# The norm's sums by way of DRAM, two transfers a chunk, and the roots one part of a turn later

## The chip, the cores and the metric

The kernel runs on one core of one Trainium2 chip. The metric is the device time of a whole execution in microseconds (us).

## The reference

Four images of 96 channels and 128 x 128 pixels go through two layers. The first layer is a state-space block: a projection to 192 channels, a depthwise convolution, SiLU, four scans along the pixels, and then a norm over the 192 channels of each pixel, a projection back to 96 channels and the residual. The second layer is a block of convolutions with an attention among channels. The change lies in the norm that ends the first layer. Cut to that, the reference is:

```python
yn = jnp.moveaxis(ym, 1, -1)                 # ym: the sum of four scans, [image, 192, 128, 128]
mu = yn.mean(-1, keepdims=True)
var = yn.var(-1, keepdims=True)
yn = (yn - mu) * jax.lax.rsqrt(var + 1e-05) * ln_w + ln_b
yn = jnp.moveaxis(yn, -1, 1)
return jnp.einsum('bdhw,cd->bchw', yn, out_w) + out_b[None, :, None, None]
...
x = x + _L0_conv_ref(_gn(x), ...)
```

## The kernel before

**The norm.** `ssm_output` makes one image's norm in 16 chunks of 1024 pixels (`SN`), each of two halves of 512 (`CH`). The mean over the channels is folded into the output weights `outws`, so that only the factor 1/sqrt(var + eps) of each pixel is needed beside the projection. A chunk goes these ways:

- `load_y` (L951, L953): SP loads the chunk's 192 channels from `yms` as `y` (128 channels) and `yr` (64 channels, the two halves one below the other).
- `squares` (L959): ACT makes the squares of `y` (part 0) and of `yr` (part 1).
- `sums` (L970): PE sums the values and the squares over the channels, with a matrix of 1/192 of 32 columns. The four results, mean and mean square of each half, stand in one PSUM bank at partitions 0, 32, 64 and 96.
- `rows` (L982, L984, L989): ACT copies the bank to `st` (L984 in image 0, L982 in the others, where the pixels are put into another order on the way), and then four DMAs from ACT's queue bring the four rows of 512 to the tile `mq`, 32 partitions x 2 x 32, where the arithmetic on them is short.
- `inverse` (L996 to L998): three short operations of DVE make the variance. `roots` (L1002): ACT takes the root. `back` (L1006, L1008, L1010): DVE takes the reciprocal, POOL's queue stores it to the DRAM tile `rd`, and SP loads the residual `xr`. `spread_out` (L1016): POOL's queue loads it as `r`, 96 partitions all alike.
- `projected` (L1023, L1028): PE multiplies the chunk by the output weights, into two banks. `scaled` (L1037, L1039): DVE multiplies a bank by `r`, which frees it. `added` (L1045, L1047): POOL adds `xr`, to which ACT had added the bias (L1092). `counted` (L1051): DVE's statistics for the next layer. L1098: SP stores the chunk to `xnew`.

**A turn.** The loop at the end of `ssm_output` has 18 turns. Turn c works on three chunks: the new one c (squares, sums, rows), the middle one c - 1 (from the inverse to `r`) and the old one c - 2 (projection to store). A turn has six parts, each ended by a `yield` with a cost.

**The order.** `ssm_output` is a generator. `co_run` runs two generators by turns, by their costs: `left`, and beside it `light` or `last`. The norm of image 0 runs as `left` beside the last part of the scan (`ssm_scan`: softplus L676, exponentials L809, DVE's scan L837, L854, L858, POOL's products L833 and L866). The norms of images 1, 2 and 3 run as `light` beside the convolutions of the image before (L2169, L1477 and others). `in_order(first)` ties every engine's instructions from the first projection on, image 0's norm included, to the order in which the program emits them. What is emitted after it, the norms of images 1 to 3 with it, is arranged by the framework, which takes the order of emission as a priority and puts an instruction where it takes it to be ready. Each engine then runs its own queue in order, and an instruction that waits holds up all behind it.

**Buffers.** `mq`, `r` and `xr` have two buffers each, `st` one, `y` and `yr` three. The PSUM pool of the norm has three banks in image 0 and two in images 1 to 3; `projected` takes two and `sums` one.

Of the kernel before, what the change touches and what calls it, by code (L numbers as in the profile page):

```python
# [9 lines left out]
F32 = mybir.dt.float32  # L10
# [10 lines left out]
CH = 512  # L21
# [11 lines left out]
TN = W // TW  # L33
# [38 lines left out]
def kernel(  # L72
# [26 lines left out]
    nc = tc.nc  # L99
# [4 lines left out]
    dram = ctx.enter_context(tc.tile_pool(name="dram", bufs=2, space=DRAM))  # L104
# [45 lines left out]
    for q in range(2):  # L150
        at = 32 * q + 16
# [137 lines left out]
    def bank(ps):  # L289

        return ps.tile([128, CH], F32, name="bank", tag="bank")

    def part(ps, *shape):
        n = 1
        for d in shape[1:]:
            n *= d
        t = bank(ps)[: shape[0], :n]
        return t if len(shape) == 2 else t.rearrange("p (a b) -> p a b", b=shape[2])
# [636 lines left out]
    def ssm_output(b, yms, xnew, stats, ps, side, turned):  # L935

        with tc.tile_pool(name="c2", bufs=2, side=side) as p2:
            xb = x[b].rearrange("c h w -> c (h w)")
            rd = dram.tile([L], F32, name="rd")
            ys, sums_of, near, made = {}, {}, {}, {}

            def load_y(c):
                if c < NS:
                    y, rest = ys[c] = [
                        p2.tile([128, n], F32, name=m, bufs=3) for m, n in (("y", SN), ("yr", CH))
                    ]  # L950
                    nc.sync.dma_start(y, yms[0:128, bass.ts(c, SN)])  # L951
                    for h in range(2):
                        nc.sync.dma_start(  # L953
                            rest[64 * h : 64 * h + 64], yms[128:192, bass.ts(2 * c + h, CH)]
                        )

            def squares(c, j):
                sq = p2.tile([128, CH if j else SN], F32, name=f"sq{j}")
                nc.scalar.activation(sq, ys[c][j], AF.Square)  # L959
                sums_of[c, j] = sq  # L960

            def sums(c, j):
                sq = sums_of.pop((c, j))
                if j == 0:
                    sums_of[c] = bank(ps)
                pm = sums_of[c]
                for g in range(4):
                    rhs = sq if g % 2 else ys[c][j]
                    p = slice(64 * (g // 2), 64 * (g // 2) + 64) if j else slice(0, 128)
                    nc.tensor.matmul(  # L970
                        pm[32 * g : 32 * g + 32],
                        lhsT=mean192[p],
                        rhs=rhs[p, :] if j else rhs[:, bass.ts(g // 2, CH)],
                        start=(j == 0),
                        stop=(j == 1),
                    )
            def rows(c):
                st = p2.tile([128, CH], F32, name="st", bufs=1)
                pm = sums_of.pop(c)
                if turned:  # L980
                    to = st.rearrange("p (h j t) -> p h j t", j=TW, t=TN)
                    nc.scalar.copy(to, turned_view(pm))  # L982
                else:
                    nc.scalar.copy(st, pm)  # L984
                mq = made[c] = p2.tile([SN // TN, 2, TN], F32, name="mq")
                for i in range(2):
                    for h in range(2):
                        at = 32 * i + 64 * h
                        nc.scalar.dma_start(  # L989
                            mq[16 * h : 16 * h + 16, i],  # L990
                            st[at : at + 1].rearrange("p (a f) -> p a f", f=TN),
                        )

            def inverse(c):
                m, q = made[c][:, 0], made[c][:, 1]
                nc.vector.tensor_mul(m, m, m)  # L996
                nc.vector.tensor_sub(q, q, m)
                nc.vector.tensor_scalar(q, q, 0.0, None, ALU.max)  # L998

            def roots(c):  # L1000
                q = made[c][:, 1]
                nc.scalar.activation(q, q, AF.Sqrt, bias=eps[0 : SN // TN])  # L1002

            def back(c):
                q = made.pop(c)[:, 1]
                nc.vector.reciprocal(q, q)  # L1006
                to = rd[bass.ts(c, SN)]
                nc.gpsimd.dma_start(to.rearrange("(p f) -> p f", f=TN), q)  # L1008
                xr = p2.tile([C, SN], F32, name="xr")
                nc.sync.dma_start(xr, xb[:, bass.ts(c, SN)])  # L1010
                near[c] = xr, to

            def spread_out(c):
                xr, to = near[c]
                r = p2.tile([C, SN], F32, name="r")
                nc.gpsimd.dma_start(r, to.partition_broadcast(C))  # L1016
                near[c] = xr, r

            def projected(c):
                po = [part(ps, C, CH) for _ in range(2)]  # L1020
                y, rest = ys.pop(c)
                for h in range(2):
                    nc.tensor.matmul(  # L1023
                        po[h], lhsT=outws[:, 0], rhs=y[:, bass.ts(h, CH)], start=True, stop=False
                    )
                for h in range(2):
                    p = slice(64 * h, 64 * h + 64)
                    nc.tensor.matmul(  # L1028
                        po[h], lhsT=outws[p, 1], rhs=rest[p], start=False, stop=True
                    )  # L1030
                return po

            def scaled(c, h, po):
                r = near[c][1][:, bass.ts(h, CH)]
                if turned:
                    v = r.rearrange("p (h j t) -> p h j t", t=TN, j=TW)
                    nc.vector.tensor_mul(v, turned_view(po), v)  # L1037
                else:
                    nc.vector.tensor_mul(r, po, r)  # L1039

            def added(c, h):
                xr, r = (t[:, bass.ts(h, CH)] for t in near[c])
                if turned:
                    v = r.rearrange("p (h j t) -> p h j t", t=TN, j=TW)
                    nc.gpsimd.tensor_add(v, v, turned_view(xr))  # L1045
                else:
                    nc.gpsimd.tensor_add(xr, r, xr)  # L1047

            def counted(c, h):
                t = near[c][turned]  # L1050
                nc.vector.bn_stats(stats[:, 2 * c + h], t[:, bass.ts(h, CH)])  # L1051

            for c in range(3):
                load_y(c)
            yield 2.0
            for c in range(NS + 2):
                new, old = c < NS, c - 2 if c >= 2 else None
                mid = c - 1 if 1 <= c <= NS else None
                if old is not None:
                    po = projected(old)  # L1060
                if mid is not None:
                    inverse(mid)
                if new:
                    squares(c, 0)
                yield 1.2
                if mid is not None:
                    roots(mid)
                if old is not None:
                    scaled(old, 0, po[0])
                if new:  # L1070
                    squares(c, 1)
                yield 1.4
                if mid is not None:
                    back(mid)
                if old is not None:
                    added(old, 0)
                    scaled(old, 1, po[1])
                if new:
                    sums(c, 0)
                yield 1.4  # L1080
                if new:
                    sums(c, 1)
                if old is not None:
                    added(old, 1)
                    counted(old, 0)
                    load_y(c + 1)
                yield 1.4
                if new:
                    rows(c)
                if mid is not None:  # L1090
                    xr = near[mid][0]
                    nc.scalar.activation(xr, xr, AF.Identity, bias=outbs)  # L1092
                    spread_out(mid)
                if old is not None:
                    counted(old, 1)
                yield 1.4
                if old is not None:
                    nc.sync.dma_start(xnew[:, bass.ts(old, SN)], near.pop(old)[turned])  # L1098
                yield 1.4
# [176 lines left out]
    def turned_view(v):  # L1276

        return v.rearrange("p (h t j) -> p h j t", t=TN, j=TW)
# [1310 lines left out]
    at = Attention(psl, d1, d2, pm)  # L2589
# [108 lines left out]
```

## Time and profile before

| what | value |
|---|---|
| median of three runs | 6406.59 us (6383.12 to 6412.63) |
| the profiled execution | 6409.68 us, its span 6407.8 us |
| PE, DVE, ACT, POOL busy | 82%, 73%, 59%, 51% of the span |
| norm of image 0, first to last copy `st` | 2105.6 to 2329.2 us |
| norms of images 1, 2, 3, first to last copy `st` | 3248.3 to 3496.4, 3964.1 to 4182.4, 4789.6 to 5005.4 us |
| DMAs `mq<-st` on ACT's queue | 256, 2.0 KB each |

PE is the matmul engine (TensorE), PEld its weight load, DVE the VectorE, ACT the ScalarE, POOL the GpSimd, SP the SyncE, which here only issues DMAs. A "q" behind an engine means its instruction queue. In a table by stretches each engine has its busy us and, in brackets, its number of instructions; then come the granted share of PE's clock, the share of the DMA engines in use and GB/s. A row of waits names who waited for whom, the us in total, how many times, and the longest. A row of a timeline has start, duration, engine, line, operation, output<-inputs, shapes, and in square brackets the idle time of the engine before it and what ended it. A row with three numbers between slashes gives the least, median and greatest duration in ns; then the first and last start in us.

### The profile page before, as it was taken

The page shows a single profiled execution, that of the slowest core. Times are in us where ns is not written, and L with a number is a line of the kernel's source. Part 1 is how long each engine was busy: PE and PEld are TensorE (multiplying, and loading weights), DVE is VectorE, ACT ScalarE, POOL GpSimd, SP SyncE. Part 2 cuts the span into 40 slices and gives each one's busy share as a digit, 9 for nine tenths or more (in the row PEclk, how much of TensorE's full clock was granted, in tenths as well). Part 3 has the DMA queues.
Part 4 walks back from the last instruction along what each step waited for, and adds up shares of the span by engine and source line. Part 5 has one row for each costly group of instructions (what it writes and reads, how often), then busy time and mean ns, then how long its engine had stood idle before and what let it go on. Part 6 is the DMA issues. An engine that isn't in the chain of part 4 may idle for free. (4 is left out here: it accounts for less than half of the span.)

```text
span 6407.8 us, 76468 instructions
## 1 busy us (share of the span) xinstructions
PE 5253.4 (82%) x23264; PEld 2254.8 (35%) x23264; DVE 4699.9 (73%) x7132; ACT 3759.4 (59%) x4770; POOL 3238.6 (51%) x2476
## 2 busy tenths in 40 slices
PE   6889988987888643989988588977888877889888
PEld 2333322322222111444433234345333444345553
DVE  4247878988989768989844686468774687988767
ACT  1247767787787666777622465466644665545642
POOL 1326757978879554979822234436304365022310
PEclk9899989998999765999999799989989888999989
DMA  6766777775675766676667686665776656967668
GB/s 155 175 160 189 198 199 199 214 221 163 198 202 171 202 183 207 196 213 179 182 185 195 166 228 163 195 169 156 214 199 184 175 149 165 245 167 180 191 168 221
DMA packets 897706, 1205.30 MB, mean 188 GB/s; under 512 B 230644, under 2 KB 745642, under 8 KB 884816
## 3 DMA queue, kind: packets, MB, share of 16 engines
q1 hardware_dynamic: 866640, 1145.36, 65.5%
q0 software_dynamic: 16336, 38.51, 2.3%
q10 hardware_dynamic: 14320, 16.54, 0.9%
q8 instruction: 187, 3.06, 0.2%
q14 instruction: 223, 1.83, 0.1%
HBM read 777.82 MB, written 345.62 MB: 175 GB/s over the span
## 5 line engine op out<-in xcount | busy, mean ns | idle before, releaser
L633 PE MATMUL bank<-y,wp 128*128 128x512 f32 (+3 forms) x3584 | 1310.9, 622 | 83.8 <-DMA y<-y 41.0
L866 POOL TENSOR_TENSOR y<-y,dl 128x1024 f32<-128x1024 f32 x384 | 1058.5, 2757 | 263.0 <-DVE dl L858 240.3
L833 POOL TENSOR_TENSOR dl<-dl,u 128x1024 f32<-128x1024 f32 x384 | 1008.8, 2627 | 253.1 <-ACT dA L809 121.1
L854 DVE TENSOR_TENSOR_SCAN dA<-dA,pBC 128x512 f32<-128x512 f32 x768 | 981.6, 1278 | 30.7
L2169 PE MATMUL bank<-y,wn 128*64 128x384 f32 (+5 forms) x2408 | 680.1, 507 | 58.3 <-DMA y<-x1d 34.1
L1477 PE MATMUL two<-ya,wd 128*64 128x192 f32 (+3 forms) x2376 | 582.2, 414 | 174.0 <-ACT odd L1550 65.1
L633 PEld LDWEIGHTS bank<-y,wp 128*128 128x128 f32 (+3 forms) x3584 | 456.2, 168 | 749.3 <-issue 651.1
L858 DVE TENSOR_TENSOR dl<-dA,pBC 128x512 f32<-128x512 f32 x768 | 528.5, 688 | 255.8 <-PE pBC L747 183.8
L747 PE MATMUL pBC<-xr,wbc 60*128 60x512 bf16 (+1 forms) x1536 | 457.8, 404 | 311.5 <-DVE dA L854 239.1
L1938 ACT COPY yb<-ya 64x768 f32<-64x768 f32 (+1 forms) x660 | 537.7, 815 | 195.5 <-PE two L1477 113.8
L676 ACT ACTIVATE dl<-pd,dtb 128x512 f32<-128x512 f32 x768 | 485.5, 684 | 187.9 <-PE pd L747 171.5
L1477 PE MATMUL two<-yb,wd 128*64 128x192 f32 (+3 forms) x2376 | 559.0, 400 | 4.0 <-ACT yb L1938 4.0
L837 DVE TENSOR_TENSOR pBC<-dl,pBC 128x512 f32<-128x512 f32 x768 | 527.5, 687 | 8.8 <-POOL dl L833 7.8
L2169 PEld LDWEIGHTS bank<-y,wn 128*64 128x64 f32 (+3 forms) x2408 | 310.3, 169 | 357.2 <-issue 186.2
L809 ACT ACTIVATE dA<-dl,negA 128x1024 f32<-128x1024 f32 x384 | 420.3, 1141 | 2.3
L1477 PEld LDWEIGHTS two<-ya,wd 128*64 128x64 f32 (+1 forms) x2376 | 262.2, 165 | 370.9 <-ACT odd L1550 75.0
L676 ACT ACT_TABLE_LOAD x248 | 318.2, 1283 | 91.9 <-PE pd L747 79.7
L747 PEld LDWEIGHTS <-wbc 60*128 60x128 bf16 (+1 forms) x1536 | 103.1, 96 | 752.1 <-issue 739.3
L1477 PEld LDWEIGHTS two<-yb,wd 128*64 128x64 f32 (+1 forms) x2376 | 289.7, 167 | 150.5 <-issue 42.1
L1477 PE MATMUL two<-ya,wa 128*96 128x384 f32 (+1 forms) x528 | 231.2, 521 | 72.9 <-DMA ya<-vp 27.0
L1550 ACT COPY odd<-two 128x384 f32<-128x384 f32 (+5 forms) x176 | 115.8, 658 | 291.3 <-PE two L1492 179.1
L1406 POOL TENSOR_TENSOR pl<-x 96x256 f32<-96x256 f32 (+3 forms) x396 | 275.2, 710 | 0.0
(322 smaller groups left out, 9105.4 us busy)
## 6 DMA issues: line engine op xcount, KB each, us to landing
u<-zb SPq DMA_DIRECT2D x192, 1024.0 KB
yms<-y SPq DMA_DIRECT2D x96, 512.0 KB
xn<-xnew SPq DMA_DIRECT2D x128, 384.0 KB
ya<-vp SPq DMA_DIRECT2D x120, 336.0 KB
y<-y SPq DMA_DIRECT2D x128, 258.2 KB
zb<-z SPq DMA_DIRECT2D x64, 512.0 KB
y<-yms SPq DMA_DIRECT2D x64, 512.0 KB
ya<-x1p SPq DMA_DIRECT2D x90, 336.0 KB
```

What stands on the lines that cost most here:

```text
L633: nc.tensor.matmul(blocks(pz[p:e]), lhsT=ws[k][:, d, c : c + e - p], rhs=window(ys[k], at, d, n), start=(i == 0), stop=(i == len(terms) - 1),)
L676: nc.scalar.activation(dst, src, AF.Softplus, bias=bias)
L747: nc.tensor.matmul(p, lhsT=w[rows], rhs=xr[rows, at : at + CH], start=True, stop=True)
L809: nc.scalar.activation(live[m]["dA"], live[m]["dl"], AF.Exp, scale=negA[:, g % 3, k : k + 1])
L833: nc.gpsimd.tensor_mul(t, t, u_view(n))
L837: nc.vector.tensor_mul(p, live[n]["dl"][:, bass.ts(half, CH)], p)
L854: nc.vector.tensor_tensor_scan(h, h, p, init, ALU.mult, ALU.add)
L858: nc.vector.tensor_mul(live[n]["dl"][:, sl], live[n]["dA"][:, sl], live[n]["C", half])
L866: nc.gpsimd.tensor_add(v, v, t.rearrange("p (a b) -> p a b", b=W))
L1477: nc.tensor.matmul(of(to[p:e], r), lhsT=w[:, i, c : c + e - p], rhs=tiles(t[k][PAIR[i]][:, SLOT[i]], o, r), start=(k == 0), stop=False,)
L1938: nc.scalar.copy(yb[k][64 * h - 64 : 64 * h, :, :n], ya[k][0:64, :, h * TN : h * TN + n])
L2169: nc.tensor.matmul(pc[p:e, :n].rearrange("p (h w) -> p h w", w=W), lhsT=w[:, c : c + e - p], rhs=v[:, :, 0:W], start=(i == 0), stop=(i == ...
```

## The change

The sums of a chunk go from `st` to a DRAM tile of 4 x 512 in one DMA, and from there to `mq` in a second one, both on ACT's queue. For that the rows of the bank are put into another order: first the two means, then the two mean squares. There are two such DRAM tiles, taken by turns. In a turn `inverse` moves from part 1 to part 2, `roots` from part 2 to part 3, and `back`, with its reciprocal, its store to `rd` and its load of `xr`, from part 3 to part 4. `spread_out` stays in part 5.

```diff
@@ ssm_output
             rd = dram.tile([L], F32, name="rd")
+            sums_to = [dram.tile([4, CH], F32, name=f"sums{i}") for i in range(2)]
...
                 for g in range(4):
-                    rhs = sq if g % 2 else ys[c][j]
-                    p = slice(64 * (g // 2), 64 * (g // 2) + 64) if j else slice(0, 128)
+                    rhs = sq if g // 2 else ys[c][j]
+                    h = g % 2
+                    p = slice(64 * h, 64 * h + 64) if j else slice(0, 128)
                     nc.tensor.matmul(
                         pm[32 * g : 32 * g + 32],
                         lhsT=mean192[p],
-                        rhs=rhs[p, :] if j else rhs[:, bass.ts(g // 2, CH)],
+                        rhs=rhs[p, :] if j else rhs[:, bass.ts(h, CH)],
...
                 mq = made[c] = p2.tile([SN // TN, 2, TN], F32, name="mq")
-                for i in range(2):
-                    for h in range(2):
-                        at = 32 * i + 64 * h
-                        nc.scalar.dma_start(
-                            mq[16 * h : 16 * h + 16, i],
-                            st[at : at + 1].rearrange("p (a f) -> p a f", f=TN),
-                        )
+                nc.scalar.dma_start(sums_to[c % 2], st[0:128:32])
+                nc.scalar.dma_start(
+                    mq, sums_to[c % 2].rearrange("(i h) (a f) -> (h a) i f", i=2, f=TN)
+                )
...
                 if old is not None:
                     po = projected(old)
-                if mid is not None:
-                    inverse(mid)
                 if new:
                     squares(c, 0)
                 yield 1.2
                 if mid is not None:
-                    roots(mid)
+                    inverse(mid)
                 if old is not None:
                     scaled(old, 0, po[0])
                 if new:
                     squares(c, 1)
                 yield 1.4
                 if mid is not None:
-                    back(mid)
+                    roots(mid)
                 if old is not None:
                     added(old, 0)
                     scaled(old, 1, po[1])
                 if new:
                     sums(c, 0)
                 yield 1.4
+                if mid is not None:
+                    back(mid)
                 if new:
                     sums(c, 1)
```

## The prediction

> **What bounds the kernel now.** I first took the stretches table over the four times in which the norm (`ssm_output`) runs, one for each image: from its first to its last copy of sums (row L984, then L982).
>
> ```profile
> core 0: us, PE busy (x) PEld busy (x) DVE busy (x) ACT busy (x) POOL busy (x), PEclk, DMA share, GB/s
> 2105.00:2340.00 235.00, 153.86 (x464) 31.39 (x461) 155.91 (x217) 146.76 (x169) 121.12 (x89) 0.77 0.71 211
> 3245.00:3505.00 260.00, 220.10 (x832) 80.06 (x832) 101.34 (x225) 75.36 (x120) 58.60 (x58) 0.93 0.69 187
> 3960.00:4190.00 230.00, 209.25 (x1179) 86.28 (x1176) 108.70 (x240) 109.21 (x153) 81.90 (x106) 0.99 0.66 183
> 4785.00:5015.00 230.00, 206.71 (x1113) 83.45 (x1112) 103.51 (x234) 105.99 (x150) 90.90 (x119) 0.96 0.68 192
> ```
>
> Only 955 of 6407.8 us hold any work of this change, so 0.5% (32 us) is 3.4% of the place where it can act, or 0.5 us in each of 64 turns. In images 1 to 3 PE is busy 85 to 91%: PE sets the time there, and a wait on another engine counts only where PE then waits. In image 0 no engine stands out: the waits decide.
>
> ```profile
> PE bank L970 <- ACT sq L959: 54.2, 15, 7.5
> ACT xr L1092 <- DMA mq<-st: 32.2, 10, 5.8
> ACT st L984 <- PE bank L970: 25.4, 12, 3.6
> ```
>
> This is the table of waits from 2105 to 2340. PE waits mainly for the squares that ACT makes. ACT's 146.8 us leave out its DMA issues; 64 of them at 0.602 us (the row below) are 38.5 us more, 185 of 235. So **ACT's queue sets image 0's turn**, 14.9 us (2105.6 to 2329.2 in 15 turns). ACT's timeline shows one turn:
>
> ```profile
> 2206.35 0.58 ACT L984 COPY st<-bank 128x512 f32<-128x512 f32 x1 [2.04 <-PE bank L970]
> 2206.97 2.43 ACTq L989 DMA_DIRECT2D mq<-st  x4
> 2209.50 1.15 ACT L1092 ACTIVATE xr<-xr,outbs 96x1024 f32<-96x1024 f32 x1 [2.56 <-DMA mq<-st]
> 2210.56 1.04 ACT L959 ACTIVATE sq<-y 128x1024 f32<-128x1024 f32 x1
> 2211.62 1.28 ACT L676 ACT_TABLE_LOAD   x1
> 2212.91 1.27 ACT L676 ACTIVATE dl<-pd,dtb 128x512 f32<-128x512 f32 x2
> 2214.20 1.28 ACT L1002 ACT_TABLE_LOAD   x1
> 2215.49 0.32 ACT L1002 ACTIVATE mq<-mq,eps 32x32 f32<-32x32 f32 x1
> 2215.72 0.61 ACT L959 ACTIVATE sq<-yr 128x512 f32<-128x512 f32 x1
> 2218.37 0.59 ACT L984 COPY st<-bank 128x512 f32<-128x512 f32 x1 [2.04 <-PE bank L970]
> ```
>
> ACT is never idle except 2.04 us before the copy `st`, where PE sums the squares it has just made. Before L1092 stand the 2.43 us of four issues. The root stands ahead of the second squares, so its 1.60 us (table load and 0.32) delay them and the sums. Next, the waits table of image 1 (3245 to 3505):
>
> ```profile
> DVE mq L996 <- DMA mq<-st: 65.1, 14, 8.6
> PE bank L970 <- DVE r L1037: 20.7, 6, 7.9
> DVE r L1037 <- DMA r<-rd: 11.2, 4, 3.8
> ```
>
> DVE waits long for the sums, but what reaches PE is only its wait for `scaled` (r L1037), which frees the PSUM bank. The same PE row is 9.8 and 9.0 us in images 2 and 3: 39.5 us together. Read back from those waits on the timeline, DVE had stood at L996 before some of them and at the landing of `r<-rd` before about as many.
>
> **What the Trainium skill says.** "DMA: Bandwidth & Descriptors", section "Two DMAs through the same engine are not ordered": a DMA that reads what another wrote must have its issuing engine wait for the first one's semaphore. The trace agrees: POOL's issue of `r<-rd` waits for `rd<-mq`, 21.4 us in nine times in image 0. So ACT will stand between its two issues. The same page, "Issuing engines are not separate DMA queues": all issuers share the 16 DMA engines, so a small transfer can stand behind SP's. The trace agrees: in its packet records, the last packet of a turn's four `mq<-st` ended 0.80 us at the least after the last issue, 2.10 in image 0's mean, 4.31 at most, 1.50 in the mean of images 1 to 3.
>
> **The change part by part, image 0.** There the issue order is that of the program.
>
> ```profile
> L989 ACTq DMA_DIRECT2D mq<-st x256: 508/602/1947, 2106.2 to 5008.3; - x128
> ```
>
> - Two issues in place of four: 2 x 0.602 = 1.2 us in place of 2.4, so 1.2 less a turn.
> - The wait between them, W, isn't in the trace. From below: the quickest write of like size to DRAM is `rd<-mq`,
>
> ```profile
> L1008 POOL DMA_DIRECT2D rd<-mq x64: 496/518/544, 2114.3 to 5013.6; - x64
> DMA to landing us min/median/max: 1.6/4.2/8.3
> ```
>
> 1.6 us with its 0.5 us of issue, so 1.1. From above: its median less the issue, 3.7. The queue of ACT is hardware and its packets in image 0 ended 2.1 us after the issue; a DRAM landing adds 0.3 (1.1 against 0.8, the two minima), but four rows go in place of 64 pieces. I take W = 2.3. Behind it on ACT wait L1092, both squares, softplus and the exponentials, and PE waits for those.
> - Net on ACT: 2.3 - 1.2 = +1.1 a turn, 16 turns, **+18 us**; bounds -2 and +40.
> - L1092 waits in any case: its rows in the waits table (32.2, 6.5, 3.7, 2.6 and 2.5 us in 15 waits) hold 15 x 2.43 of issue, and the rest, 11 us, is mostly the load of `xr`. W runs beside that: **-8 us** (0 to -11). The load's issue on SP moves one part later with `back`, past SP's rows and stores of the scan; it stood there for its buffer anyway (in the timeline SP issued the store that frees it at 2195.69 and this load at 2201.49, 8 us ahead of L1092), so I count that at nothing; if the cover of 8 us is gone, L1092 waits for it, by at most a part, 2.5 us.
> - The root moves behind the second squares into the 2.04 us hole. Twelve turns have such a hole (25.4 us); 1.5 us each, **-18 us**. From the other side, 0, if a softplus of the scan fills the hole or DVE's inverse is late.
> - The sums' new order lets two matmuls in place of one go before the squares are there. PE's hole of 2 us gets shorter by part of a matmul; the root covers it: nothing.
> - DVE and POOL: the inverse one part later takes away DVE's stand at L996 (15.5 us of waits, and inside the instruction: 2.57 us at 2210.25 where the median is 0.18). DVE is busy 66% and ACT hardly waits for it (4.1 us): nothing. POOL gets `rd<-mq` one part later, so `r<-rd` waits longer for its landing, by about the 2.5 us of a part; POOL is busy 52% and now idles as long at L1008. The scan's POOL products behind it cover with their lead; if that is gone, DVE waits for `dl`.
>
> Image 0: 18 - 8 - 18 = **-8 us**, from -31 to +40.
>
> **Images 1 to 3, 48 turns.** Here the order in the trace is not the program's: r L1037 stands between L996 and L997, which the program emits in a row. So "one part later" may move little. The sums reach SBUF after 0.6 + 1.8 (1.50 + 0.3) + 0.6 + 1.8 = 4.8 us, before 2.4 + 1.5 = 3.9: 0.9 later, against a part of 14.9/6 = 2.5. DVE's waits for them are 65.1 + 8.9, 45.2 + 7.9 and 51.5 + 5.1 = 184 us, 3.8 a turn; 1.6 a turn goes, 77 us, of which PE feels 39.5/184: -16. The factor `r` lands 1 to 2 us later; DVE's waits for it were 11.2 + 9.7 + 11.8 us in twelve turns, eight turns more at 1.5 us, half of it reaching PE: +6. ACT stands some 1.1 us longer, but it idles over half of these stretches, and PE waits for ACT's squares, `odd` and `kt` 19 us in all: +6 at a guess of a tenth of the 53 us. Sum **-4 us**; bounds -40 (all of PE's wait for `scaled`) and +40 (three quarters of ACT's 53 us).
>
> **Sum.** -8 - 4 = -12 us. The profiled execution took 6409.7 us, its span 6407.8, and 2 us lie around it; it is 3 us above the median shown, 6406.6. I subtract from the median: **6395 us**.
>
> **Rivals.**
> 1. *Landing under load becomes ACT's wait* (slower). Place: ACT between its two issues. For it: the landing of 4.2 us at the median, a DMA share of 0.71, a first packet that began up to 3.8 us after the issue. Image 0 +40; in images 1 to 3 PE waits for ACT and for a late `r`, +10: 6457. It decides from W = 2.8 us on, where 1.2 saved and (18 + 8)/16 = 1.6 are used up. Against it: the quickest landings of 1.1.
> 2. *DVE's stand at the sums was on PE's path* (faster). Then nearly all of the 39.5 us goes, and image 0 comes near its -8 with W small: 39.5 + 8 = 47 less: 6359. For it: DVE's 184 us. Against it: `r<-rd` stood before half of those waits.
> 3. *The change doesn't do what it says*: the order of images 1 to 3 puts the inverse right after the sums again, the parts move nothing and the extra trip through DRAM makes `r` late. +10 there and -8 in image 0: 6409.
>
> **How the numbers follow.** 0.5% is about what a measurement of this kernel can tell from no change (the three runs lie 29 us apart). Forecast 0.37, rival 3 0.06, rival 2 0.31, rival 1 0.26. A tenth of the forecast's own range goes over on the faster side and rival 1 may stop short: faster 0.34, same 0.41, slower 0.25. The range goes from a little beyond rival 2, 6347, to rival 1, 6457; forecast's own 6374 to 6438.
>
> **What the profile after would show.** Right: two rows of ACT issues of 64, and ACT idle about 2 us between them; L1002's table load between the second squares and `st`, and the wait `st` <- PE near 5 us; DVE's mq waits down from 184 to about 110 us; image 0's turn at 14.4 us. Wrong: a stand of over 3 us on ACT between the issues, PE waiting for squares for over 54 us, or DVE r <- `r<-rd` doubled to over 65 us.

## The result, and the profile after

The changed kernel takes 6431.69 us in the median of nine runs, the kernel before, on the same chip, 6405.73 us: the ratio is 1.0052, with a 95% interval of 1.0038 to 1.0066. A second measurement of the same kernel (`e9_change_again`) gave 1.0058 (1.0037 to 1.0078). So the change makes the kernel slower by half a per cent, 26 to 37 us, where the forecast had it 12 us faster. The profiled execution took 6430.42 us, its span 6428.6, 20.8 more than before.

In the changed kernel the lines stand elsewhere: squares L960, sums L972, the copy `st` L986 (L984 in images 1 to 3), the two transfers L988 and L989, inverse L995 to L997, root L1001, reciprocal L1005, `rd` L1007, `scaled` L1036 and L1038, bias L1091.

First the table of stretches, over the same four times as before.

```profile
core 0: us, PE busy (x) PEld busy (x) DVE busy (x) ACT busy (x) POOL busy (x), PEclk, DMA share, GB/s
2105.00:2340.00 235.00, 147.60 (x471) 30.18 (x469) 142.52 (x211) 143.94 (x168) 121.30 (x89) 0.77 0.72 208
3245.00:3505.00 260.00, 225.34 (x834) 80.53 (x834) 99.37 (x214) 71.68 (x114) 58.99 (x56) 0.93 0.67 186
3960.00:4190.00 230.00, 200.00 (x1096) 81.63 (x1094) 101.55 (x227) 98.70 (x139) 77.99 (x102) 0.96 0.64 175
4785.00:5015.00 230.00, 205.82 (x1029) 82.59 (x1028) 114.68 (x236) 99.61 (x139) 74.36 (x99) 0.93 0.67 186
```

The reader should look at the number of matmuls. In image 2, 1096 of them fall into 230 us in place of 1179, in image 3 1029 in place of 1113: the same work runs later. In image 0 DVE gets through 211 instructions in place of 217.

The waits of image 0 (2108 to 2347: who waited for whom, us in total, times, the longest):

```profile
PE bank L972 <- ACT sq L960: 50.8, 14, 9.0
ACT xr L1091 <- DMA sums<-st: 47.5, 11, 7.9
ACT st L986 <- PE bank L972: 15.3, 8, 3.3
```

ACT's wait for PE's sums at `st` went from 25.4 to 15.3, as intended, but the row ahead of L1091 went from 32.2 (four issues) to 47.5 (one issue and a stand), with its rows of other causes from 51.0 to 71.5. One turn on ACT's timeline shows the stand:

```profile
2206.90 0.61 ACT L960 ACTIVATE sq<-yr 128x512 f32<-128x512 f32 x1
2207.53 1.28 ACT L1001 ACT_TABLE_LOAD   x1
2208.83 0.32 ACT L1001 ACTIVATE mq<-mq,eps 32x32 f32<-32x32 f32 x1
2209.14 0.59 ACT L986 COPY st<-bank 128x512 f32<-128x512 f32 x1
2209.75 0.50 ACTq L988 DMA_DIRECT2D sums<-st  x1
2215.02 0.31 ACTq L989 DMA_DIRECT2D mq<-sums  x1
2215.43 1.15 ACT L1091 ACTIVATE xr<-xr,outbs 96x1024 f32<-96x1024 f32 x1 [5.71 <-DMA sums<-st]
```

The root stands behind the second squares and in this turn the hole ahead of `st` is gone (no idle time in brackets). Then ACT ends the first issue at 2210.25 and begins the second at 2215.02: a stand of 4.77 us. Over the 16 turns of image 0 this stand is 3.66 us in the mean (1.24 to 6.88). In images 1 to 3 2.4 to 2.6 us lie between the two issues, but in 25 of 48 chunks the framework put other work between them; ACT is idle 1.3 to 2.0 us in the mean just ahead of the second. The issues themselves are shorter than the 0.602 us of before (least, median, greatest in ns):

```profile
L988 ACTq DMA_DIRECT2D sums<-st x64: 501/502/1061, 2109.3 to 5032.5; - x64
L989 ACTq DMA_DIRECT2D mq<-sums x64: 309/322/376, 2111.8 to 5037.2; - x64
```

In image 1 (waits from 3245 to 3515):

```profile
DVE mq L995 <- DMA mq<-sums: 46.1, 12, 8.9
DVE r L1036 <- DMA r<-rd: 24.9, 5, 7.4
PE bank L972 <- DVE r L1036: 14.4, 6, 5.6
```

Over images 1 to 3, in the same three windows of both profiles (3245 to 3515, 3960 to 4215, 4780 to 5060), DVE's waits for the sums fell from 186 to 123 us (46.1, 40.4, 36.5), and its waits for the factor `r` rose from 41 to 85 (24.9, 31.7, 28.2). PE's wait for `scaled` did not move: 38.7 us (14.4, 17.5, 6.8), before 39.5. These are single executions: the seven profiles whose order in these images is that of before (`before`, `e1`, `e6`, `e7`, `e8`, `e15`, `e18`) have 143 to 186 us of waits for the sums, and `before` has the most.

### The profile page after: what moved, and what is told of

The parts are those of the page before. It is cut to its first block, busy times and chain, and to the rows that moved or that the text cites. A ratio compares the mean times of both kernels' runs of the same rounds, so it can differ in the third digit from the quotient of the medians.

```text
span 6428.6 us, 76281 instructions
## 1 busy us (share of the span) xinstructions
PE 5252.6 (82%) x23264; PEld 2253.8 (35%) x23264; DVE 4692.6 (73%) x7132; ACT 3758.9 (58%) x4770; POOL 3241.7 (50%) x2476
## 5 line engine op out<-in xcount | busy, mean ns | idle before, releaser
L2168 PE MATMUL bank<-y,wn 128*128 128x384 f32 (+5 forms) x2408 | 676.0, 506 | 62.9 <-DMA y<-x1d 30.1
L2168 PEld LDWEIGHTS bank<-y,wn 128*128 128x128 f32 (+3 forms) x2408 | 308.3, 168 | 357.2 <-issue 180.3
## 6 DMA issues: line engine op xcount, KB each, us to landing
ya<-vp SPq DMA_DIRECT2D x120, 336.0 KB
ya<-x1p SPq DMA_DIRECT2D x90, 336.0 KB
```

The costliest lines, as they stand in the source:

```text
L2168: nc.tensor.matmul(pc[p:e, :n].rearrange("p (h w) -> p h w", w=W), lhsT=w[:, c : c + e - p], rhs=v[:, :, 0:W], start=(i == 0), stop=(i == ...
```

## The experiments

The theories that the expectations name are these. STAND: ACT's stand between the two transfers costs the time. LATE: the numbers come later (`mq`, then `r` and the load of `xr`). RING: an old chunk's buffers come free too late. ORDER: the framework arranges the instructions of images 1 to 3 anew, and the arrangement it made for the kernel before was a good one. Each run is told by its ratio to the kernel before. Beside it I use the length of a stretch of PE's work between the same two matmuls in every profile, which shows where time was lost; it is worked out from the traces and comes from one execution each.

**Where, and which half.** The whole change in image 0 alone, and in images 1 to 3 alone (`turned` is true there; the diff is that of `e1` against the changed kernel, `e2` has the opposite condition):

```diff
-                nc.scalar.dma_start(sums_to[c % 2], st[0:128:32])
...
+                if not turned:
+                    nc.scalar.dma_start(sums_to[c % 2], st[0:128:32])
...
+                else:
+                    for i in range(2):
+                        for h in range(2):
...
-                    inverse(mid)
+                    (roots if turned else inverse)(mid)
...
-                    roots(mid)
+                    (back if turned else roots)(mid)
```

> The whole change (two transfers by way of DRAM, the sums' order, the parts) in image 0 alone, where the order of issue is that of the program; images 1 to 3 go the way of the kernel before. In the profile after, ACT stood 3.7 us in the mean between its two issues in image 0, and the place had lost 5 us. Theory STAND (ACT's wait between the issues delays what is behind it): +5 us or more, up to +17 if the profile's 5 us were lucky; PE's wait for the squares in image 0 over 54 us. Theory LATE (the loss is that r comes late and holds the PSUM banks in images 1 to 3): within 4 us of the kernel before. Theory ORDER (the framework arranges images 1 to 3 otherwise, by luck): anything within 15 us, by what it rearranges behind image 0.

> The whole change in images 1 to 3 alone; image 0 goes the way of the kernel before. The profile after put about 20 of its 26 us here, 14 of them in image 2. STAND: with the framework's filling between the two issues, +5. LATE: +15 to +25, with DVE's wait for r<-rd at 65 us or more in place of 33. ORDER: a number that doesn't go together with image 0's to make 26.

Measured: 1.0012 (1.0004 to 1.0021) in image 0 alone, 1.0024 (1.0015 to 1.0033) in images 1 to 3 alone. Both places lose; a third of the two lies in image 0. Together they make 0.36%, less than the 0.52 and 0.58% of the whole.

Then the two halves of the change over all images. `e3` has the transfers by DRAM and the order of the sums as in the change, and the parts of before; `e4` has the four transfers and the sums of before, and the moved parts, its whole diff against before:

```diff
-                    inverse(mid)
...
-                    roots(mid)
+                    inverse(mid)
...
-                    back(mid)
+                    roots(mid)
...
+                    back(mid)
```

> The two transfers by way of DRAM with the sums' order that goes with them, and inverse, roots and reciprocal in the parts of the kernel before. STAND: as slow as the whole change or slower, +26 to +45, since the root is ahead of the second squares again and ACT still stands. LATE: less than the whole change, about +10, since a part's delay of r is taken back: DVE's wait for r<-rd falls towards 45 us. ORDER: between 0 and +40.

> Four transfers on chip as before, and inverse, roots and reciprocal one part later. STAND: a gain, 10 to 18 us, from the root in the hole before the copy of the sums in image 0, and DVE no longer standing at the sums. LATE: a loss of about 10, since r comes a part later without the trip. ORDER: between -15 and +15.

Measured: 1.0031 (1.0019 to 1.0042) and 1.0019 (1.0010 to 1.0027). Neither half is free, and 0.31 + 0.19 = 0.50% is about the whole. But each of them also makes the framework arrange images 1 to 3 anew. I counted in the traces the instructions that stand at another place in their engine's order than before (DMA issues left out; an expectation below counts in another way): there `e3` has 359 of DVE and 196 of ACT, `e4` 218 and 148, the change 431 and 238. So these four runs can't tell a step from what the framework makes of it.

**Steps alone, in which images 1 to 3 stay put.** In the kernel before, `e6` issues `spread_out` one part later (the first diff), `e7` has the root behind the second squares (the second), and `e8` the new order of the sums (the third):

```diff
-                    spread_out(mid)
...
+                if mid is not None:
+                    spread_out(mid)
```

```diff
-                if mid is not None:
-                    roots(mid)
...
                 if new:
                     squares(c, 1)
+                if mid is not None:
+                    roots(mid)
```

```diff
-                    rhs = sq if g % 2 else ys[c][j]
+                    rhs = sq if g // 2 else ys[c][j]
```

> The kernel before, with spread_out (POOL's load r<-rd) in part 6 in place of 5; it moves eight rows of POOL in image 0 and nothing else. LATE: DVE's wait for r<-rd in image 0 rises from 5 us towards 25, and the kernel loses 3 to 10 us (1.0005 to 1.0015). STAND: no change.

> The kernel before, with the root behind the second squares within part 2; it moves 30 rows of ACT in image 0 and nothing else, and r comes only 0.6 us later. If the prediction's step of the hole holds (1.5 us in twelve turns): 10 to 18 us faster, 0.9972 to 0.9984. If the root in the hole brings nothing: 0.9995 to 1.0005.

> The kernel before, with only the new order of the sums (both values, then both squares) and the four transfers on chip to match. The order on DVE, ACT and SP stays; PE's differs within the sums. STAND, LATE: no change, within 0.05%. ORDER (luck of PE's order): anything to 0.2%.

Measured: 1.0005 (0.9992 to 1.0017), 0.9999 (0.9989 to 1.0009), 0.9997 (0.9988 to 1.0007): three times nothing. In images 1 to 3 no instruction of DVE or ACT stands elsewhere in the three traces. In `e7` the hole does close in some turns. ACT's timeline there:

```profile
2188.26 1.15 ACT L1092 ACTIVATE xr<-xr,outbs 96x1024 f32<-96x1024 f32 x1 [8.23 <-DMA mq<-st]
...
2196.78 0.61 ACT L959 ACTIVATE sq<-yr 128x512 f32<-128x512 f32 x1
2197.41 1.28 ACT L1002 ACT_TABLE_LOAD   x1
2198.71 0.32 ACT L1002 ACTIVATE mq<-mq,eps 32x32 f32<-32x32 f32 x1
2199.43 0.58 ACT L984 COPY st<-bank 128x512 f32<-128x512 f32 x1 [0.40 <-PE bank L970]
```

The idle time ahead of `st` is 0.40 us here and not 2.04, but a turn earlier ACT idles 8.23 us ahead of the bias, 2.43 of them issues. What ACT gains at one place it waits out at the next. Over the image (2105 to 2340) its largest rows are:

```profile
ACT xr L1092 <- DMA mq<-st: 25.8, 7, 8.2
ACT st L984 <- PE bank L970: 16.0, 7, 3.9
```

The wait at `st` went from 25.4 to 16.0 us, and that ahead of the bias, with all its causes and the issues, from 47.5 to 57.8. All of ACT's waits together stayed: 86.3 us before, 86.6 in `e7`.

**The stand.** In the changed kernel the second transfer goes one part later, behind the bias (`e5`, `rows_back` issues it); or SP issues it in place of ACT (`e10`).

```diff
                 rows(c)
...
                 yield 1.4
+                if new:
+                    rows_back(c)
```

```diff
-                nc.scalar.dma_start(
+                nc.sync.dma_start(
                     mq, sums_to[c % 2].rearrange("(i h) (a f) -> (h a) i f", i=2, f=TN)
```

> The whole change, with the second transfer (mq<-sums) issued at the start of part 6, behind the bias on ACT (L1091), in place of right behind the first. In image 0 ACT then works through part of the landing; in images 1 to 3 the order of instructions hardly differs from the change's. STAND: 5 to 12 us faster than the change (1.0033 to 1.0044 of the kernel before). LATE: no faster, 1.0052 or above, since mq lands later still.

> The whole change, with the second transfer (mq<-sums) issued by SP in place of ACT: SP takes over the stand until the first has landed, and ACT has one issue of 0.5 us and no stand. STAND: half or more of the loss goes, 1.001 to 1.003. LATE: none of it goes, 1.005, since the sums reach mq no sooner. Both theories lose if SP's stand holds up its loads: above 1.007.

Measured: 1.0034 (1.0020 to 1.0047) and 1.0194 (1.0171 to 1.0217). On SP the whole loses nearly four times as much. I take it that the second transfer stands there ahead of SP's loads; but 1430 instructions of DVE stand elsewhere than in the change, so the run doesn't part the one from the other. `e5` is the cleaner one: in its trace every instruction of DVE, POOL and SP, and ACT's computing, stand where they do in the change, and only the second transfers of image 0 stand later. It is 0.2% faster than the change (1.0052 and 1.0058), what STAND had expected, though the intervals overlap.

**More buffers.** A third buffer (of `xr` in image 0, of `r` in images 1 to 3) in the kernel before and in the changed one, beside the change itself once more:

```diff
-                xr = p2.tile([C, SN], F32, name="xr")
+                xr = p2.tile([C, SN], F32, name="xr", bufs=2 if turned else 3)
...
-                r = p2.tile([C, SN], F32, name="r")
+                r = p2.tile([C, SN], F32, name="r", bufs=3 if turned else 2)
```

> The change itself once more, beside the three others of this set, so that they stand beside it on one chip. 1.004 to 1.0066 of the kernel before, by every theory.

> The kernel before with a third buffer for the tile that is stored at the end of the norm (xr in image 0, r in images 1 to 3). Theory RING (image 0's turn is set by the ring load of xr, bias on ACT, residual on POOL, store, buffer free, next load, and not by ACT's own work, which would explain why the root in the hole brought nothing): 6 to 20 us faster, ACT's wait for xr in image 0 gone. Without RING: within 0.1%.

> The change with that third buffer. RING with LATE (a late r hurts through the ring: added late, stored late, the next xr late, ACT standing at L1091): nearly all of image 0's loss goes, and with it a third of the whole, 1.001 to 1.0035. STAND alone: 1.004 or above, as the change, or by as much better than it as the kernel before gains from the third buffer.

Measured: the change 1.0058 (1.0037 to 1.0078), with the buffers 1.0050 (1.0031 to 1.0069): RING, which had 1.001 to 1.0035 for it, falls. The surprise is the kernel before with a third buffer: **1.0035** (1.0018 to 1.0052). A buffer that can only take waits away makes it slower. Its waits in image 3 (4780 to 5060):

```profile
DVE mq L996 <- DMA mq<-st: 17.3, 6, 7.9
...
PE bank L970 <- DVE r L1037: 7.2, 4, 2.5
```

The same rows in the kernel before:

```profile
DVE mq L996 <- DMA mq<-st: 51.5, 12, 7.0
...
PE bank L970 <- DVE r L1037: 9.0, 5, 2.5
```

DVE waits 17.3 us for the sums, where the kernel before waited 51.5, and PE 7.2 for `scaled` in place of 9.0. Fewer waits, and yet slower: so the length of DVE's waits for the sums does not tell the time. What the buffer also changed is the order: 541 instructions of DVE and 189 of ACT stand elsewhere.

**The order held.** To part a step from its arrangement, I tied each engine's instructions in images 1 to 3 to an order given as a list: that of a finished program. These dependencies set the order alone, not a wait on the chip (`e15` has them all, has no instruction of DVE elsewhere than before, and gives 0.9993).

```diff
+    def hold(made):
...
+            order = [own[k + d] for k, d in enumerate(places)]
+            for a, b in zip(order, order[1:]):
+                tc.add_manual_dep(
+                    b, a.name, mybir.DependencyInfo(
+                        mybir.DependencyClass.NoSync, mybir.DependencyReason.DATA
+                    ), reason="order held")
```

`e13` is `e3` in the order of the kernel before; `e14` is the kernel before in the order of `e3`; `e15` is `e11` in the order of the kernel before; `e16` is `e13` with image 0 as before.

> The sums by way of DRAM in all four images and nothing else of the change (as in e3_trip_only, which gave 1.0031), but in images 1 to 3 the instructions of every engine are held in the order that the framework chose for the kernel before; on VectorE, GpSimd and SyncE not one row stands elsewhere than before, on ScalarE two transfers stand where the first and the last of four stood. ORDER (images 1 to 3 lose because the framework arranges them anew): the loss in images 2 and 3 (+6 and +9 us in e3) is gone, ratio 0.999 to 1.0015. STAND (ScalarE's wait between the two transfers is what costs): the stand is here behind no other work, so as much as in e3 or more, 1.003 to 1.006. LATE (the numbers come later): as e3, about 1.003.

> The kernel before, with all its four transfers a chunk on the chip, no transfer by DRAM and no part moved; but in images 1 to 3 the instructions of every engine are held in the order that the framework chose for e3_trip_only (414 rows of VectorE, 266 of ScalarE, 71 of GpSimd, 34 of SyncE stand elsewhere than before). ORDER: as slow as e3 in images 2 and 3, ratio 1.002 to 1.0035. STAND and LATE: there is no stand and nothing is later, 1.000 within 0.001.

> The kernel before with a third buffer (of xr in image 0, of r in images 1 to 3), as in e11_before_three (1.0035), but images 1 to 3 held in the order of the kernel before: no row stands elsewhere on any engine. ORDER: 1.000 within 0.001, since the third buffer cost only what the framework made of it. If the place of the buffers or the buffer itself costs: 1.002 to 1.0045, as in e11.

> As e13_trip_held, but image 0 is as before: the sums go by way of DRAM in images 1 to 3 alone, held in the order of the kernel before. It is the candidate for a version faster than both: ScalarE issues two transfers in place of four in 48 chunks (0.4 us less each, 19 us of ScalarE) and VectorE's waits for mq are to fall as in the changed kernel (184 to 123 us). ORDER: 0.997 to 1.000. STAND: 1.002 to 1.005, since the stand is bare. LATE: 1.002 to 1.003.

Measured, beside what was measured above:

```
                      order of before                  order of its own or of e3
four transfers        1                                e14 1.0039 (1.0024 to 1.0054)
two by way of DRAM    e13 1.0090 (1.0074 to 1.0106)    e3  1.0031 (1.0019 to 1.0042)
third buffer          e15 0.9993 (0.9980 to 1.0006)    e11 1.0035 (1.0018 to 1.0052)
```

`e14` contains nothing of the change, no trip and no moved part, and is as slow as `e3`: **the arrangement alone costs 0.4%**, and within it the trip costs nothing more. `e15` has the buffer without the arrangement, and its loss is gone. ORDER is shown for `e3` and for `e11`. But ORDER had expected `e13` at no loss, and it is the slowest of the four: 1.0090 (`e16`, in images 1 to 3 alone, 1.0090 too). In the order of before the trip costs nearly three times what it costs in the framework's own. DVE's wait for the sums in image 3 of `e13`, and of `e14`, both from 4780 to 5060:

```profile
DVE mq L1115 <- DMA mq<-sums: 87.7, 15, 12.5
```

```profile
DVE mq L1118 <- DMA mq<-st: 30.2, 5, 9.9
...
PE bank L1092 <- DVE r L1159: 9.8, 4, 4.7
```

In the order of before DVE stands at the inverse, waiting for `mq`, in 37 of 48 chunks (the 14, 11 and 12 times of its rows in images 1, 2 and 3). With the trip these waits are 238 us in images 1 to 3 in place of 186 (the rows of the inverse's first two lines in the same three windows): 52 us over 48 chunks, 1.1 us each, near the 0.9 that the prediction gave for the later arrival. The agreement is rough, since the other profiles in the order of before start from as little as 143 us. What stands behind the inverse on DVE comes later by that, and, as I read it, ACT's root and POOL's store with it.

**Stand or lateness, and image 0.** In `e17` the second transfer of `e16` stands up to three instructions further on in ACT's order. In `e18`, the change in image 0 alone, it is issued one part later, as in `e5`, and images 1 to 3 stay as before.

```diff
                 yield 1.4
+                if new and not turned:
+                    rows_back(c)
```

> As e16_trip_later_held (DRAM in images 1 to 3 alone, order of the kernel before, 1.009), but the second transfer stands on ScalarE up to three instructions further on, as far as they ran before VectorE's inverse of the chunk in the kernel before (none in 10 of 48 chunks, one in 9, two in 10, three in 19), so that the stand is filled with other work. Nothing else stands elsewhere. STAND (ScalarE's bare stand made e16's 0.9%): 0.999 to 1.003. LATE (mq lands later, and VectorE, which stands at the inverse soon after in this order, with it: its waits for mq rose from 162 to 238 us in images 1 to 3 of e13): as e16, 1.006 to 1.010.

> The whole change in image 0 alone, as in e1_image0 (1.0012; image 0 some 12 us longer), but the second transfer is issued one part later, behind the addition of the bias to xr. Images 1 to 3 are as before, in their order too. STAND: image 0 at or below that of the kernel before (305 us in the mean of the unchanged ones), ratio 0.998 to 1.000; it is also a candidate for a version faster than both. If what image 0 lost was the moved roots and the later load of xr: as e1, 1.001 to 1.002.

Measured: `e17` 1.0118 (1.0101 to 1.0134), worse than the bare stand. ACT's stand is shorter but not gone: just ahead of the second transfers it idles 77 us in sum, in `e16` 98. `mq` comes later still (DVE's waits 273 us, in `e16` 237), and the time goes up with `mq`. That points to LATE, and not to STAND, for what `e13` and `e16` pay in images 1 to 3; no run there parts the two fully. `e18` 1.0011 (1.0001 to 1.0021), where `e1` gave 1.0012: ACT idles 33 us ahead of the second transfers of image 0 in place of 63, and by the time that saves nothing that can be told. The waits of image 0 in `e18` show where it went:

```profile
ACT xr L1104 <- DMA xr<-in_x: 40.2, 8, 8.3
PE bank L972 <- ACT sq L960: 38.3, 12, 7.1
PE pBC L747 <- DVE dA L854: 36.2, 11, 8.8
```

ACT now waits 40.2 us for the load of `xr`, which was issued a part later with `back`; in the kernel before that row was 6.5 us. PE's wait for the squares fell (57.4 in `e1`), but its wait for DVE's `dA` of the scan rose (22.4 in `e1`, 15.8 before).

**Where the time lies.** Lengths of the same stretches of PE's work in us, the mean and, in brackets, the least and greatest. The stretches are named by their times in the kernel before: image 0 from 2095 to 2400, image 2 from 3945 to 4240, image 3 from 4770 to 5100.

```
image 0: as before there (before, e2, e14, e16, e17)                 307.8 (304.9 to 311.8)
         one step alone (e6, e7, e8)                                 302.5 (301.3 to 304.9)
         parts alone (e4)                                            307.0
         trip alone (e3, e13)                                        310.0 (308.2 to 311.9)
         whole change (after, e1, e9, e12)                           317.9 (313.4 to 320.3)
         whole change, second transfer later (e5, e18)               310.0 (309.0 to 310.9)
image 2: order of before (before, e1, e6, e7, e8, e15, e18)          294.7 (290.0 to 297.3)
         arranged anew (after, e2 to e5, e9, e11, e12, e14)          306.6 (298.7 to 313.4)
         order of before with the trip (e13, e16, e17)               315.7 (310.3 to 323.4)
image 3: order of before                                             327.3 (323.9 to 330.5)
         arranged anew                                               335.2 (332.2 to 342.1)
         order of before with the trip                               363.3 (357.9 to 368.5)
```

In images 2 and 3 none of the nine profiles that are arranged anew is as short as the longest in the order of before, whatever was changed in them: 12 and 8 us in the mean. Image 1, from 3230 to 3600, shows no such difference (369.9 in the order of before, 367.7 anew). Four profiles have the change's own arrangement in images 1 to 3, `after`, `e2`, `e5` and `e9`: 306.2 in image 2 and 336.0 in image 3. Between 5100 and 6300, in work of the second layer after the last norm, they are 5 us shorter (1194.6 against 1199.6 in the order of before); that gain is in three of the four and not in `e5` (1200.7), and I didn't find its cause. Together the change gives +10 (image 0), +11 and +9 (images 2 and 3), and -5: +25, against 26 to 37 measured.

## Why the prediction was wrong, point by point

**ACT's issues and W (+18).** The direction was right. The term was mis-sized: two issues take 0.50 + 0.32 = 0.8 us and not 1.2, but W is 3.66 us and not 2.3, so the net is 3.66 + 0.82 - 2.43 = 2.05 a turn, +33 over 16 turns and within the bounds given. W is 2.5 to 2.8 us in image 0 of the two kernels with the trip alone and 3.7 to 4.0 in the four with the moved parts as well. In the latter the load of `xr` lies more often just ahead of the first transfer: its nearest issue on SP is 3.8 to 6.5 us ahead in 9 of 16 turns of the profile after, and 5.0 to 6.8 us ahead in 4 turns of `e3`. That this load delays the small transfer is argued, not shown.

**L1092's cover (-8).** The cover is there: of the +33, only 10 us reach PE's work in image 0. But the load of `xr` that moves one part later was counted at nothing. With the parts alone (`e4`) ACT waits 17.0 us for it, and image 0 is no longer for that; with the stand cut by half (`e18`) it waits 40.2 us. So I read that stand and load hide one another; the whole change with the load at its old place was not run. Moving the second transfer shortens the stretch from 318 to 310; in `e5` the time points the same way, in `e18` it doesn't.

**The hole ahead of `st` (-18).** This step failed outright. `e7` takes 9 us of the 25.4 away with this step alone, and the time is 0.9999. I had taken ACT's queue as full, with the hole as its only idle time, from one turn of the timeline; in the turn before it ACT waited 4.55 us ahead of L1092, of which 2.43 are issues. In `e7` the freed time went there (47.5 to 57.8 us), so ACT's own work alone does not set image 0's turn.

**DVE and POOL in image 0 (nothing).** Nothing speaks against it: the parts alone leave image 0 at 307.0 against 307.8, in one execution.

**Images 1 to 3, DVE's waits (-16).** The number came nearly as forecast, 186 to 123 us where I had 184 to 107, but not its price. I had given DVE's waits a share of PE's waits, 39.5 of 184 us. `e11` (83 us of such waits) and `e14` (104) wait less than the kernel before and are slower, so there is no such rate. Where `mq` comes later in an unchanged order (`e13`), on the other hand, 52 us more of these waits (95 against the least of the seven profiles) came with 58 us more of time. I read it so: a wait that the arrangement takes away by moving the waiting instruction is paid back at another place, one that a late transfer makes is not. The first half of that is not shown.

**`r` later (+6).** The sign that I had named for the wrong case, DVE's waits for `r<-rd` doubled to over 65 us, came true: 85, in windows where the kernel before had 41 (70 in `e9`, the same kernel again). PE's wait for `scaled` nevertheless stayed at 39 us.

**ACT's stand in images 1 to 3 (+6).** Not told: PE's waits for the norm's squares rose from 4.4 to 9.9 us, near the guess, but `e11` and `e14`, which have no stand, have 14.2 and 10.5. The new arrangement alone can make that rise.

**What no term had.** I wrote that the order of images 1 to 3 "is not the program's", and concluded that the parts may move little there. The arrangement did not stay, 431 instructions of DVE stand elsewhere in these images, and no rearrangement was priced. Together with the hole that is the step behind the wrong sign: images 2 and 3 are 20 us longer in the change where all three images were forecast at -4, and image 0 is 10 us longer where it was forecast at -8. That such a loss comes of the arrangement is shown for `e3` and `e11`, by `e14` and `e15`; for the whole change I conclude it, since its lengths there are those of the other new arrangements, and no version of it with the order held was run.

**The rivals.** Rival 1 had the sign, and its deciding point, W over 2.8 us in image 0, was passed. Of its 40 us in image 0 10 came, and in images 1 to 3 nothing points to ACT's stand; `e13` shows what the later `mq` would have cost there in the old arrangement. Rival 2 falls with `e11` and `e14`. Rival 3 falls, since the parts did move the instructions of images 1 to 3. The range held the measured time; that is luck, since the gains at the hole and at DVE's waits did not come.

**What stays open.** What sets image 0's turn, and why the arrangements cost what they do. In image 2 the change has PE idle longer (49.4 us in the stretch against 36.1, busy 260.5 against 260.6). In image 3 it is PE's busy time for the same 1564 matmuls that grew (289.1 against 282.6, idle 43.2 against 44.2) at a lower granted clock (0.909 against 0.929). No version that beats the kernel before came out of these runs.

## What to carry to other kernels

Where a scheduler arranges instructions by its own model, an edit, even one more buffer, can also draw a new arrangement; hold the old order, or hold the new order without the edit, before you believe that a step costs or saves. A wait counts by what comes later because of it, not by its length: price it by moving the result it waits for in an order that stays the same. And two transfers that depend on one another on a computing engine's queue cost their landing under load, so count what that stand hides before you take it away.

## What was unexpected of the hardware

In image 3 PE paid for a wait twice. In the seven profiles in the order of before it was idle 42 to 48 us in the stretch, and its busy time was 281 to 286 us at a granted clock of 0.917 to 0.934. In the three with the trip in that same order (`e13`, `e16`, `e17`) it was idle 61 to 65 us, and busy 297 to 304 us for as many matmuls at a clock of 0.866 to 0.886. So 18 us of waiting came with 18 us of slower matmuls in the mean. The Trainium skill, "TensorE: Matmul & The Clock Gate", section "What's actually happening", says that the clock is set by how busy PE has been recently; this stretch agrees. But it is no fixed price: the same kernels have 13 us more idle and 8 us more busy time in image 2, 7 and 1 us in image 1, and the changed kernel's clock in image 3 is lower (0.909) with no more idle time.

A dependent write and read of 8 KB by way of DRAM held ACT 1.0 us at best (`e9`) and up to 6.9 us at a DMA share of 0.7. In image 0 the stand, 3.66 us in the mean, outweighed the 1.6 us of issues that it saved.
